# Moving a small weight product, nine small loads, the head masks and the per-batch norms in a two-layer attention and expert kernel

## The chip, the cores and the metric

The kernel runs on one core of one Trainium2 chip. The core has five engines that take their instructions in program order and meet through semaphores: TensorE (PE for matmuls, PEld for its weight loads), VectorE (DVE), ScalarE (ACT), GpSimd (POOL) and SyncE (SP), which only issues DMAs. The metric is the device time in microseconds of one execution; the median of the runs is what counts.

## What is computed

The input x has 8 batches of 512 rows of 128 numbers, all in float32. Two layers follow each other, each of the form x + layernorm(f(layernorm(x))).

```python
def layer1(x):                       # one head of width 128, causal
    q, k, v = rope(x @ wq), rope(x @ wk), x @ wv
    p = softmax(mask(q @ k.T / 128))   # the scale enters once with q and once with k
    return (p @ v) @ wo

def layer2(x):                       # 16 heads of width 4, then 8 experts, 2 chosen per row
    h = rmsnorm(x, g1); c = h @ w_down
    q, k, v = rope(c @ wq), rope(c @ wk), c @ wv
    x = x + softmax(causal(q @ k.T / 2)) @ v @ w_up
    t = rmsnorm(x, g2)
    gate = top2(softmax(t @ router_w))   # two largest, renormalised
    return x + sum(gate[e] * ((silu(t @ w1[e]) * (t @ w3[e])) @ w2[e]) for e in range(8))

x = x + layernorm(layer1(layernorm(x)))
x = x + layernorm(layer2(layernorm(x)))
```

## The kernel before, in words

**Staging.** A batch is 4 tiles of 128 rows. x stays in SBUF (`x_all`), and so do the results of both layers (`h_all`) and all weights. The work has three stages: the "wide" attention of layer 1, batch by batch; the "narrow" attention of layer 2 in units of four heads (class `Unit`, `period`); and the experts. Each stage is begun inside the one before. Most of the order is written out by hand: within `tc.manual_schedule()` each engine's instructions stand in the order in which the Python code emits them, and generators (`prepare`, `fill`, `ffn_front`, `period`) are advanced a step at a time by `step()`. Code outside of such blocks is ordered by a scheduler.

**The start.** SP issues the loads of x (batch 0, then the rope table `ropea`, then batches 1 to 7) and then the expert weights w1s, w3s, w2s (L82 to L111). ACT issues six loads for `wqk`, then `wv` and `wo` (L92 to L100). POOL issues nine small loads, `wdown`, three for `wqkv`, `wup`, `wr`, `g1c`, `g2c`, `ropef` (L391 to L405), and makes the masks: `mask_a` for the wide scores, `mask_q` and `mask_k` for the narrow ones, and `order` for the routing (L409 to L445).

**The norm of x.** `stats_x(b)` (L228) takes the moments of batch b on DVE (`bnst_x`, `mv_x`, `ve_x`), then `root_x` and two small operations for `shift_x` on POOL. `Wide.norm` (L240) has ACT write the four normed tiles `xn`; `Wide.turn` (L253) transposes them on PE and ACT copies `xnT` out of PSUM.

**The projection product.** `fuse_projections` (L208) multiplies wv and wo into `wvo` and takes each row's mean off: a PE transpose, an ACT copy (`wvT`), a PE matmul, three DVE operations. `values` needs `wvo`.

**The wide loop.** `wide_attention` (L994) has 9 rounds (b = 0 to 8) of four phases, with a `yield` after each. In round b, batch b is projected and scored, batch b - 1 gets its probabilities transposed and weighed, and batch b - 2 (only batches 0 to 2) is finished. The methods:

- `project(i)` (L258): PE writes `pq`, DVE multiplies it with the rope table (`two`), POOL adds the halves (`roped`).
- `turn_probs` (L308): PE transposes the probabilities of tiles 0 and 1, then of 2, then of 3 into PSUM (`pT_ps`), and ACT copies each to `pT`.
- `values` (L269): PE writes `pv`, ACT copies `v`. `weigh` (L322): ten PE products `pr`, then on DVE `rinv` and the product into `h_all`.
- `scores(half)` (L282): PE writes two tiles of scores and adds the mask `mask_a`; DVE takes `nmax` and ACT the exponentials `p` of each tile in turn.
- `norm_result` (L343): moments of `h_all` on DVE (`bnst_r`, `ve_r`), then `root_r` on POOL. `add` (L346): four DVE operations that add the normed result to `x_all`. `norm_sum` (L368): moments of the new `x_all` on DVE (`bnst_h`, two `ve`), then four POOL operations for `h_scale`, by which layer 2 norms its input.

The phases of a round were

```
1: norm(b+1), norm_result(b-2), project(b, 0), turn_probs(b-1; 0, 1), project(b, 1)
2: [round 0: fuse_projections], turn_probs(b-1; 2), (3), add(b-2), values(b), norm_sum(b-2)
3: weigh(b-1), stats_x(b+2), turn(b+1), scores(b, first half)
4: scores(b, second half)
```

After each phase the driver (L1052 to L1064) advances other generators: two steps of `prepare` and `fill` in rounds 0 to 2, two steps of `first` in rounds 3 and 4, and from round 5 one step of `first` and of `fronts`; the first narrow scores (`units_begin`) start in phase 3 of round 5.

**The front of layer 2.** `first` is `front_and_rows(0)`. `ffn_front(0)` (L520) norms batch 0 on POOL (`hs`, four operations that need `h_scale`), transposes it on PE (`hT_ps`) with an ACT copy `hT`, projects it on PE (`pqk`, `pvs`) with DVE's product `two` and ACT's copy `vs`, adds the halves on POOL (`rot`), and splits the result there into three bfloat16 parts (`split`, L448: `thirds` and `left`). Six DMAs on SP store the parts to DRAM (`q_dram`, `k_dram`, L569), and `load_rows(0)` (L573) reads them back on SP as `q_rows` and `k_rows`. `Unit.rowwise` (L608) reads these rows for the first narrow scores (`sm`, L617), adds `mask_q` (L600), and DVE takes the maximum (`nm`, L632).

**PSUM.** Three double banks are shared by `pq`, `sc`, `pqk`, `sm` and the like (tag `wide`), and two banks by all transposes, `pv`, `pvs` and `pr` (tag `bank`), in the order of their allocation; one is written again only when its reader is done.

Of the kernel before, what the change touches and what calls it, by code (L numbers as in the profile page):

```python
# [15 lines left out]
P = 128  # L16
# [6 lines left out]
def kernel(  # L23
# [43 lines left out]
    def banks(stack, **bufs):  # L67

        for name, n in bufs.items():
            psum[name] = stack.enter_context(  # L70
                tc.tile_pool(name=f"ps_{name}_{n}", bufs=n, space=bass.MemoryType.PSUM)
            )
# [4 lines left out]
    def bank(name):  # L77
        return psum["bank"].tile([P, 512], F32, tag="bank", name=name)
# [3 lines left out]
    for b in range(B):  # L82
# [4 lines left out]
        if b == 0:  # L87
            ropea = const.tile([P, 2, T], F32, name="ropea")
            nc.sync.dma_start(out=ropea, in_=rope_a)


    wqk = const.tile([P, 2, 2, D], F32, name="wqk")  # L92
    for i, w in enumerate((a_wq, a_wk)):
        nc.scalar.dma_start(out=wqk[:, i, 0, :], in_=w[0])
        nc.scalar.dma_start(out=wqk[:, i, 1, 0 : D // 2], in_=w[0][:, D // 2 : D])
        nc.scalar.dma_start(out=wqk[:, i, 1, D // 2 : D], in_=w[0][:, 0 : D // 2])
    wv = const.tile([P, D], F32, name="wv")
    nc.scalar.dma_start(out=wv, in_=a_wv[0])
    wo = const.tile([P, D], F32, name="wo")
    nc.scalar.dma_start(out=wo, in_=a_wo[0])  # L100

    w1s = const.tile([P, E, F], F32, name="w1s")
    w3s = const.tile([P, E, F], F32, name="w3s")
    w2s = const.tile([P, E, FC, D], F32, name="w2s")
# [103 lines left out]
    def fuse_projections():  # L208
        ps = bank("wvo_ps")
        nc.tensor.transpose(ps[:, :P], wv, ident)  # L210
        wvT = work.tile([P, D], F32, tag="sq", name="wvT", bufs=1)
        nc.scalar.copy(wvT, ps[:, :P])
        ps = bank("wvo_ps2")
        nc.tensor.matmul(ps[:, :P], wvT, wo, start=True, stop=True)
        mean = stat.tile([P, 1], F32, tag="wvo_mean", name="wvo_mean", bufs=1)
        nc.vector.tensor_reduce(mean, ps[:, :P], AX.X, ALU.add)
        nc.vector.tensor_scalar(mean, mean, 1.0 / D, None, ALU.mult)
        nc.vector.tensor_scalar(wvo, ps[:, :P], mean, None, ALU.subtract)
# [9 lines left out]
    def stats_x(b):  # L228
        mv, rstd = ln_stats(x_all, b * NT, "x")
        x_stats[b] = minus_product(mv[:, :, 0], rstd, "shift_x", f"shift_x_{b}"), rstd  # L230
# [151 lines left out]
            h_scale[b] = kept  # L382

    batches = [Wide(b) for b in range(B)]
    with tc.manual_schedule():
        stats_x(0)
        batches[0].norm()
        stats_x(1)


    wdown = const.tile([P, L], F32, name="wdown")  # L391
    nc.gpsimd.dma_start(out=wdown, in_=w_down)
    wqkv = const.tile([L, 3, L], F32, name="wqkv")
    for i, w in enumerate((f_wq, f_wk, f_wv)):
        nc.gpsimd.dma_start(out=wqkv[:, i, :], in_=w)
    wup = const.tile([L, D], F32, name="wup")
    nc.gpsimd.dma_start(out=wup, in_=w_up)
    wr = const.tile([P, E], F32, name="wr")
    nc.gpsimd.dma_start(out=wr, in_=router_w)
    g1c = const.tile([P, 1], F32, name="g1c")  # L400
    nc.gpsimd.dma_start(out=g1c, in_=g1.rearrange("(p o) -> p o", o=1))
    g2c = const.tile([P, 1], F32, name="g2c")
    nc.gpsimd.dma_start(out=g2c, in_=g2.rearrange("(p o) -> p o", o=1))
    ropef = const.tile([P, NT, 2, HD], F32, name="ropef")
    nc.gpsimd.dma_start(out=ropef, in_=rope_f.rearrange("(t p) s d -> p t s d", p=P))  # L405
    ident_bf = const.tile([P, P], BF16, name="ident_bf")
    nc.vector.tensor_copy(ident_bf, ident)

# [9 lines left out]
        channel_multiplier=1,  # L418
    )

    def half_masks(name, sign):


        m = const.tile([P, 2, P], BF16, name=name)
        nc.gpsimd.memset(m, 0.0)
        for i in range(2):
            for h in range(2):
                at = m[i * HR : (i + 1) * HR, h, :]
                nc.gpsimd.affine_select(
                    out=at,  # L430
                    in_=at,
                    compare_op=ALU.is_ge,
                    fill=NEG_BF,
                    base=sign * HR * h,
                    pattern=[[-sign, P]],
                    channel_multiplier=sign,
                )
        return m

    mask_q = half_masks("mask_q", -1)  # L440
    mask_k = half_masks("mask_k", 1)

    order = const.tile([P, E], F32, name="order")
    for e in range(E):
        nc.gpsimd.memset(order[:, e : e + 1], float(E - e))  # L445


    def split(thirds, x, r):  # L448
# [474 lines left out]
    def step(tasks):  # L923
        while tasks:
            try:
                next(tasks[0])
                return True
            except StopIteration:
                tasks.pop(0)
# [64 lines left out]
    def wide_attention():  # L994
        for b in range(B + 1):
            u = batches[b] if b < B else None
            nxt = batches[b + 1] if b + 1 < B else None
            v = batches[b - 1] if b > 0 else None
            w = batches[b - 2] if 0 <= b - 2 < CLOSED else None
            if nxt:  # L1000
                nxt.norm()
            if w:
                w.norm_result()
            if u:
                u.project(0)
            if v:
                v.turn_probs(0, 1)
            if u:
                u.project(1)
            yield  # L1010
            if b == 0:
                fuse_projections()
            if v:
                v.turn_probs(2)
                v.turn_probs(3)
            if w:
                w.add()
            if u:
                u.values()
            if w:  # L1020
                w.norm_sum()
            yield
            if v:
                v.weigh()
            if b + 2 < B:
                stats_x(b + 2)
            if nxt:
                nxt.turn()
            if u:
                u.scores(0)  # L1030
            yield
            if u:
                u.scores(1)
            yield

    def front_and_rows(b):
        yield from ffn_front(b)
        yield
        load_rows(b)
# [4 lines left out]
    units_begin = [period(-2), period(-1)]  # L1044
    begun = period(0)
    with tc.manual_schedule():
        banks(ctx, wide=3)
        with ExitStack() as stage:
            banks(stage, bank=2)
            batches[0].turn()  # L1050
            fronts.append(front_and_rows(1))
            for i, _ in enumerate(wide_attention()):  # L1052
                b = i // 4
                if b < 3:
                    step(setup)
                    step(setup)
                elif b < 5:
                    step(first)
                    step(first)
                else:  # L1060
                    step(first)
                    step(fronts)
                    if b > 5 or i % 4 > 1:
                        step(units_begin)  # L1064
            for _ in range(6):
                step(fronts)
                step(units_begin) or next(begun)
    closes = [batches[b].close() for b in range(CLOSED, B)]
    banks(ctx, bank=1, po=1)
    with tc.manual_schedule():  # L1070
# [84 lines left out]
```

## Time and profile before

| | us |
|---|---|
| median of 4 runs | 798.65 (797.99 to 806.71) |
| the profiled execution | 799.24 |
| its span, first to last instruction | 797.5 |
| granted TensorE clock, mean | 0.988 |
| PE busy in the span | 724.9 (91%) |
| DVE, ACT, POOL busy | 491.1, 326.0, 285.5 |
| first norm of x (ACT `xn`) begins | 8.17 |
| first wide scores (PE `sc`) begin | 21.27 |
| load of the rows of batch 0 issued (SP) | 81.55 |
| first narrow scores (PE `sm`) begin | 91.00 |

A row of the trace in order of time has the start, the busy time, the engine, the line of the code, the operation, out<-in with shape and type, the count, and in brackets the idle time of the engine before it with what ended that. A "q" behind an engine's name means its queue, which issues DMAs. The rows of the windows have, for a stretch of time, the busy time of each engine, the granted clock of TensorE as a fraction of full speed, the mean busy share of the 16 DMA engines and the bytes moved.

### The profile page before, as it was taken

What the parts mean: (1) busy time and instruction counts of PE and PEld (TensorE: products, weight loads), DVE (VectorE), ACT (ScalarE), POOL (GpSimd) and SP (SyncE); (2) the same over time, 40 slices, a digit from 0 to 9 for tenths busy, and PEclk for the clock granted to TensorE, in tenths of its full rate; (3) what the DMA queues carried; (4) which work ended last, traced back from release to release, by engine and by line L of the source; (5) the groups of instructions that cost most, each with busy time, mean ns of one, the idle gap of its engine ahead of it and who ended that gap; (6) DMA issues with size and microseconds to landing.
All of it is one profiled execution on the core that took longest, in us unless ns stands there. A gap on an engine that the chain in (4) does not pass through costs nothing. (4 is left out here: it accounts for less than half of the span.)

```text
span 797.5 us, 15016 instructions
## 1 busy us (share of the span) xinstructions
PE 724.9 (91%) x5886; PEld 431.6 (54%) x5886; DVE 491.1 (62%) x1088; ACT 326.0 (41%) x507; POOL 285.5 (36%) x594
## 2 busy tenths in 40 slices
PE   4989897898988889898899889999999999999994
PEld 1657564444544444444444456665666666666663
DVE  3497667888778776768672246545464545454553
ACT  2554534565656556656567323222222222222220
POOL 7566451455868676757424300101010101010101
PEclk9999999999999999999999899999999999999998
DMA  9121304130403122314000000000000000000000
GB/s 284 34 88 36 85 11 111 37 89 3 110 15 93 31 69 56 100 25 105 20 3 3 0 1 2 14 0 14 1 14 1 14 2 13 1 14 0 14 1 13
DMA packets 29001, 30.36 MB, mean 38 GB/s; under 512 B 6148, under 2 KB 25316, under 8 KB 28932
## 3 DMA queue, kind: packets, MB, share of 16 engines
q0 software_dynamic: 5280, 14.31, 7.0%
q1 hardware_dynamic: 22500, 14.72, 6.5%
q8 instruction: 46, 0.75, 0.4%
q10 hardware_dynamic: 1152, 0.39, 0.2%
q14 instruction: 23, 0.19, 0.1%
HBM read 15.73 MB, written 11.53 MB: 34 GB/s over the span
## 5 line engine op out<-in xcount | busy, mean ns | idle before, releaser
L632 DVE TENSOR_REDUCE nm<-sm 128x2 f32<-128x1024 f32 (+2 forms) x192 | 194.4, 1043 | 35.4 <-PE sm L600 30.5
L696 ACT ACTIVATE pk<-sT 128x1024 f32<-128x1024 f32 x160 | 161.4, 1025 | 79.1 <-PE sT L600 78.6
L874 ACT ACTIVATE sil<-ph 128x512 f32<-128x512 f32 x128 | 76.3, 597 | 251.7 <-PE ph L866 231.3
L875 DVE TENSOR_TENSOR hid<-sil,ph 128x512 f32<-128x512 f32 x128 | 87.4, 687 | 124.0 <-ACT sil L874 124.0
L882 PEld LDWEIGHTS py<-w2s,hid 128*128 128x128 f32 x1024 | 124.2, 192 | 31.9 <-issue 27.4
L866 PE MATMUL ph<-tT_all,w1s 128*128 128x512 f32 x256 | 132.4, 599 | 0.0
L866 PE MATMUL ph<-tT_all,w3s 128*128 128x512 f32 x256 | 131.6, 596 | 0.0
L882 PE MATMUL py<-w2s,hid 128*128 128x128 f32 x1024 | 124.9, 275 | 1.9 <-DVE h_all L891 1.2
L169 POOL TENSOR_TENSOR root_o<-ve_o,half 128x4 f32<-128x4 f32 x8 | 8.2, 1022 | 309.8 <-DVE ve_o L186 309.8
L703 PE MATMUL po<-pk,vpad 128*32 128x512 f32 (+3 forms) x1024 | 97.9, 445 | 0.0
L891 DVE SCALAR_TENSOR_TENSOR h_all<-py,gate_all,h_all 128x128 f32<-128x128 f32 x256 | 72.0, 343 | 30.6 <-PE py L882 30.6
L866 PEld LDWEIGHTS ph<-tT_all,w3s 128*128 128x128 f32 x256 | 49.0, 191 | 62.0 <-issue 62.0
L673 PE MATMUL sT<-q_rows,k_rows 64*128 64x384 bf16 (+3 forms) x512 | 65.0, 299 | 18.7 <-DVE nm L632 13.7
L617 PE MATMUL sm<-k_rows,q_rows 61*128 61x256 bf16 (+3 forms) x512 | 70.9, 303 | 5.5 <-ACT pk L696 3.5
L866 PEld LDWEIGHTS ph<-tT_all,w1s 128*128 128x128 f32 x256 | 44.3, 193 | 31.9 <-issue 21.1
L617 PEld LDWEIGHTS <-q_rows 61*128 61x128 bf16 x512 | 23.6, 94 | 56.1 <-issue 52.0
L600 PE MATMUL sm<-ident_bf,mask_q 64*128 64x64 bf16 (+1 forms) x768 | 49.1, 199 | 0.0
L600 PEld LDWEIGHTS <-mask_q 64*128 64x128 bf16 x768 | 38.8, 96 | 11.7
L600 PE MATMUL sT<-ident_bf,mask_k 64*128 64x128 bf16 (+1 forms) x640 | 43.9, 206 | 0.0
L673 PEld LDWEIGHTS <-k_rows 64*128 64x128 bf16 x512 | 26.2, 93 | 32.3 <-issue 31.7
L451 POOL CAST m<-nm 128x16 bf16<-128x16 f32 x32 | 6.4, 201 | 86.8 <-DVE nm L632 86.7
L600 PEld LDWEIGHTS <-mask_k 64*128 64x128 bf16 x640 | 31.2, 94 | 11.1
(168 smaller groups left out, 844.8 us busy)
## 6 DMA issues: line engine op xcount, KB each, us to landing
q_dram<-thirds POOLq DMA_DIRECT2D x18, 192.0 KB, 3.2
k_dram<-thirds POOLq DMA_DIRECT2D x18, 192.0 KB, 3.7
q_rows<-q_dram POOLq DMA_DIRECT2D x12, 288.0 KB, 5.0
k_rows<-k_dram POOLq DMA_DIRECT2D x12, 288.0 KB, 6.4
q_rows<-m3T SPq DMA_DIRECT2D x192, 2.0 KB
x_all<-in_L_attn_x_dram SPq DMA_DIRECT2D x8, 256.0 KB
out_dram<-y SPq DMA_DIRECT2D x8, 256.0 KB
q_dram<-thirds SPq DMA_DIRECT2D x6, 192.0 KB
```

Source lines behind the costliest of these rows:

```text
L169: nc.gpsimd.tensor_tensor(y, x, half[:, :n], ALU.pow)
L600: nc.tensor.matmul(out[:, :, h * HR : (h + 1) * HR], which[at, h, :], ident_bf[at, at].unsqueeze(1).to_broadcast([HR, out.shape[1], HR]), ...
L617: nc.tensor.matmul(sc[:, i, c * n : (c + 1) * n], self.q[at, 2 * self.g + pair, t * P : n], self.k[at, 2 * self.g + pair, :n], start=(c == 0),
L632: nc.vector.tensor_reduce(self.nm[:, :, pairs[0] : pairs[0] + w, t], sc[:, :, : w * n].rearrange("p i (c n) -> p i c n", n=n), AX.X, ALU.m ...
L673: nc.tensor.matmul(sc[:, i, c : c + n], self.k[at, 2 * self.g + pair, j * P : (j + 1) * P], self.q[at, 2 * self.g + pair, j * P :], start= ...
L696: nc.scalar.activation(p[:, :, :c], sc[:, :, :c], AF.Exp, scale=HD**-0.5)
L703: nc.tensor.matmul(po[h * HP : (h + 1) * HP, j * P :], vpads[self.g][:, j, h, :], self.p[j, h // 2][:, h % 2, :], start=(self.g == 0 and j ...
L866: nc.tensor.matmul(ph[:, i, :], w[:, e, c * P : (c + 1) * P], tT_all[:, b, :], start=True, stop=True,)
L874: nc.scalar.activation(sil, ph[:, 0, :], AF.Silu)
L875: nc.vector.tensor_tensor(hid[:, c, :], sil, ph[:, 1, :], ALU.mult)
L882: nc.tensor.matmul(py[:, t * P : (t + 1) * P], hid[:, c, t * P : (t + 1) * P], w2s[:, e, c, :], start=(c == 0), stop=(c == FC - 1),)
L891: nc.vector.scalar_tensor_tensor(h_all[:, n, :], py[:, t * P : (t + 1) * P], gate_all[:, n, e : e + 1], h_all[:, n, :], ALU.mult, ALU.add,)
```

## The change

- `wv` and `wo` are loaded before `wqk` on ACT's queue.
- The nine small loads are issued by SP, behind x and ahead of the expert weights, and not by POOL.
- `fuse_projections` runs in two parts: its transpose and copy before the first norm, its product and DVE operations after the first `turn`; both stood in phase 2 of round 0.
- `mask_q`, `mask_k` and `order` are made at the end of phase 1 of round 0.
- `norm(b+1)` goes from the head of phase 1 to phase 2, behind the copies of `turn_probs`. `norm_result(b-2)` goes from phase 1 to phase 2, `add(b-2)` from phase 2 to the end of phase 4, behind the scores, and `norm_sum` from phase 2 of the same round to phase 2 of the next.
- `first` starts one phase later (the first phase of round 3 is left out), so that `h_scale` of batch 0 exists; all its steps, `load_rows(0)` too, come one phase later. `units_begin` stays where it was.

From round 7 on the order of every engine's instructions is as before; outside of the wide loop nothing else is changed.

```diff
@@ -88,17 +88,32 @@
             ropea = const.tile([P, 2, T], F32, name="ropea")
             nc.sync.dma_start(out=ropea, in_=rope_a)
 
+    wv = const.tile([P, D], F32, name="wv")
+    nc.scalar.dma_start(out=wv, in_=a_wv[0])
+    wo = const.tile([P, D], F32, name="wo")
+    nc.scalar.dma_start(out=wo, in_=a_wo[0])
 
     wqk = const.tile([P, 2, 2, D], F32, name="wqk")
     for i, w in enumerate((a_wq, a_wk)):
         nc.scalar.dma_start(out=wqk[:, i, 0, :], in_=w[0])
         nc.scalar.dma_start(out=wqk[:, i, 1, 0 : D // 2], in_=w[0][:, D // 2 : D])
         nc.scalar.dma_start(out=wqk[:, i, 1, D // 2 : D], in_=w[0][:, 0 : D // 2])
-    wv = const.tile([P, D], F32, name="wv")
-    nc.scalar.dma_start(out=wv, in_=a_wv[0])
-    wo = const.tile([P, D], F32, name="wo")
-    nc.scalar.dma_start(out=wo, in_=a_wo[0])
-
+
+    wdown = const.tile([P, L], F32, name="wdown")
+    nc.sync.dma_start(out=wdown, in_=w_down)
+    wqkv = const.tile([L, 3, L], F32, name="wqkv")
+    for i, w in enumerate((f_wq, f_wk, f_wv)):
+        nc.sync.dma_start(out=wqkv[:, i, :], in_=w)
+    wup = const.tile([L, D], F32, name="wup")
+    nc.sync.dma_start(out=wup, in_=w_up)
+    wr = const.tile([P, E], F32, name="wr")
+    nc.sync.dma_start(out=wr, in_=router_w)
+    g1c = const.tile([P, 1], F32, name="g1c")
+    nc.sync.dma_start(out=g1c, in_=g1.rearrange("(p o) -> p o", o=1))
+    g2c = const.tile([P, 1], F32, name="g2c")
+    nc.sync.dma_start(out=g2c, in_=g2.rearrange("(p o) -> p o", o=1))
+    ropef = const.tile([P, NT, 2, HD], F32, name="ropef")
+    nc.sync.dma_start(out=ropef, in_=rope_f.rearrange("(t p) s d -> p t s d", p=P))
     w1s = const.tile([P, E, F], F32, name="w1s")
     w3s = const.tile([P, E, F], F32, name="w3s")
     w2s = const.tile([P, E, FC, D], F32, name="w2s")
@@ -210,6 +225,7 @@
         nc.tensor.transpose(ps[:, :P], wv, ident)
         wvT = work.tile([P, D], F32, tag="sq", name="wvT", bufs=1)
         nc.scalar.copy(wvT, ps[:, :P])
+        yield
         ps = bank("wvo_ps2")
         nc.tensor.matmul(ps[:, :P], wvT, wo, start=True, stop=True)
         mean = stat.tile([P, 1], F32, tag="wvo_mean", name="wvo_mean", bufs=1)
@@ -382,27 +398,19 @@
             h_scale[b] = kept
 
     batches = [Wide(b) for b in range(B)]
+    banks(ctx, wide=3)
+    stage = ctx.enter_context(ExitStack())
+    banks(stage, bank=2)
     with tc.manual_schedule():
         stats_x(0)
+        projections = fuse_projections()
+        next(projections)
         batches[0].norm()
         stats_x(1)
-
-
-    wdown = const.tile([P, L], F32, name="wdown")
-    nc.gpsimd.dma_start(out=wdown, in_=w_down)
-    wqkv = const.tile([L, 3, L], F32, name="wqkv")
-    for i, w in enumerate((f_wq, f_wk, f_wv)):
-        nc.gpsimd.dma_start(out=wqkv[:, i, :], in_=w)
-    wup = const.tile([L, D], F32, name="wup")
-    nc.gpsimd.dma_start(out=wup, in_=w_up)
-    wr = const.tile([P, E], F32, name="wr")
-    nc.gpsimd.dma_start(out=wr, in_=router_w)
-    g1c = const.tile([P, 1], F32, name="g1c")
-    nc.gpsimd.dma_start(out=g1c, in_=g1.rearrange("(p o) -> p o", o=1))
-    g2c = const.tile([P, 1], F32, name="g2c")
-    nc.gpsimd.dma_start(out=g2c, in_=g2.rearrange("(p o) -> p o", o=1))
-    ropef = const.tile([P, NT, 2, HD], F32, name="ropef")
-    nc.gpsimd.dma_start(out=ropef, in_=rope_f.rearrange("(t p) s d -> p t s d", p=P))
+        batches[0].turn()
+        next(projections, None)
+
+
     ident_bf = const.tile([P, P], BF16, name="ident_bf")
     nc.vector.tensor_copy(ident_bf, ident)
 
@@ -418,10 +426,9 @@
         channel_multiplier=1,
     )
 
-    def half_masks(name, sign):
-
-
-        m = const.tile([P, 2, P], BF16, name=name)
+    def half_masks(m, sign):
+
+
         nc.gpsimd.memset(m, 0.0)
         for i in range(2):
             for h in range(2):
@@ -435,14 +442,16 @@
                     pattern=[[-sign, P]],
                     channel_multiplier=sign,
                 )
-        return m
-
-    mask_q = half_masks("mask_q", -1)
-    mask_k = half_masks("mask_k", 1)
-
+
+    mask_q = const.tile([P, 2, P], BF16, name="mask_q")
+    mask_k = const.tile([P, 2, P], BF16, name="mask_k")
     order = const.tile([P, E], F32, name="order")
-    for e in range(E):
-        nc.gpsimd.memset(order[:, e : e + 1], float(E - e))
+
+    def late_constants():
+        half_masks(mask_q, -1)
+        half_masks(mask_k, 1)
+        for e in range(E):
+            nc.gpsimd.memset(order[:, e : e + 1], float(E - e))
 
 
     def split(thirds, x, r):
@@ -997,28 +1006,27 @@
             nxt = batches[b + 1] if b + 1 < B else None
             v = batches[b - 1] if b > 0 else None
             w = batches[b - 2] if 0 <= b - 2 < CLOSED else None
-            if nxt:
-                nxt.norm()
-            if w:
-                w.norm_result()
+            summed = batches[b - 3] if 0 <= b - 3 < CLOSED else None
             if u:
                 u.project(0)
             if v:
                 v.turn_probs(0, 1)
             if u:
                 u.project(1)
-            yield
             if b == 0:
-                fuse_projections()
+                late_constants()
+            yield
             if v:
                 v.turn_probs(2)
                 v.turn_probs(3)
             if w:
-                w.add()
+                w.norm_result()
+            if summed:
+                summed.norm_sum()
+            if nxt:
+                nxt.norm()
             if u:
                 u.values()
-            if w:
-                w.norm_sum()
             yield
             if v:
                 v.weigh()
@@ -1031,6 +1039,8 @@
             yield
             if u:
                 u.scores(1)
+            if w:
+                w.add()
             yield
 
     def front_and_rows(b):
@@ -1044,27 +1054,25 @@
     units_begin = [period(-2), period(-1)]
     begun = period(0)
     with tc.manual_schedule():
-        banks(ctx, wide=3)
-        with ExitStack() as stage:
-            banks(stage, bank=2)
-            batches[0].turn()
-            fronts.append(front_and_rows(1))
-            for i, _ in enumerate(wide_attention()):
-                b = i // 4
-                if b < 3:
-                    step(setup)
-                    step(setup)
-                elif b < 5:
+        fronts.append(front_and_rows(1))
+        for i, _ in enumerate(wide_attention()):
+            b = i // 4
+            if b < 3:
+                step(setup)
+                step(setup)
+            elif b < 5:
+                if i % 4 or b > 3:
                     step(first)
                     step(first)
-                else:
-                    step(first)
-                    step(fronts)
-                    if b > 5 or i % 4 > 1:
-                        step(units_begin)
-            for _ in range(6):
+            else:
+                step(first)
                 step(fronts)
-                step(units_begin) or next(begun)
+                if b > 5 or i % 4 > 1:
+                    step(units_begin)
+        for _ in range(6):
+            step(fronts)
+            step(units_begin) or next(begun)
+        stage.close()
     closes = [batches[b].close() for b in range(CLOSED, B)]
     banks(ctx, bank=1, po=1)
     with tc.manual_schedule():
```

More of the change, by code (lines that the diff above doesn't have):

```diff
@@ L1009, in wide_attention @@
                 u.project(1)
+            if b == 0:
+                late_constants()
             yield
-            if b == 0:
-                fuse_projections()
             if v:
```

## The prediction

> **What bounds the kernel now.** I read the page first, then who PE waits for from 0 to 135 us, then the rows of all engines in order of time over that stretch, and last the windows with the granted clock.
>
> ```profile
> PE 724.9 (91%) x5886; PEld 431.6 (54%) x5886; DVE 491.1 (62%) x1088; ACT 326.0 (41%) x507; POOL 285.5 (36%) x594
> ...
> PE   4989897898988889898899889999999999999994
> ...
> PEclk9999999999999999999999899999999999999998
> ```
>
> PE is busy 91% of the span, and near 9 tenths or more everywhere but in the first slices; it issues in program order, so a PE instruction that waits moves all behind it. Only the first 135 us (the wide attention) are reordered by the change; after them the order of every engine is unchanged, so what is won or lost up to about 98 us is carried to the end.
>
> ```profile
> 8.17 1.65 ACT L245 ACTIVATE xn<-x_all,shift_x,root_x 128x128 f32<-128x128 f32 x4 [1.07 <-POOL shift_x L223]
> ...
> 18.69 0.29 DVE L216 TENSOR_REDUCE wvo_mean<-wvo_ps 128x1 f32<-128x128 f32 x1 [1.26 <-PE wvo_ps L214]
> ...
> 21.27 0.64 PE L291 MATMUL sc<-roped,roped 128*128 128x128 f32 x2
> ...
> 55.69 0.66 PE L317 MATMUL pT_ps<-ident,p 128*128 128x128 f32 x4 [1.46 <-ACT pT L320]
> ...
> 58.58 1.65 PE L199 MATMUL hT_ps<-ident,hs 128*128 128x128 f32 x4 [1.34 <-POOL hs L462]
> ...
> 75.23 1.16 POOL L455 TENSOR_TENSOR thirds<-left,thirds 128x512 bf16<-128x512 f32 x1
> ...
> 76.42 0.61 SPq L569 DMA_DIRECT2D k_dram<-thirds  x1
> ...
> 81.55 1.66 SPq L577 DMA_DIRECT2D q_rows<-q_dram  x2
> ...
> 83.33 1.56 SPq L577 DMA_DIRECT2D k_rows<-k_dram  x2
> ...
> 91.00 0.50 PE L617 MATMUL sm<-k_rows,q_rows 61*128 61x512 bf16 x2
> ```
>
> In these rows the first number is the start, the second the busy time, the bracket the idle time before and its releaser. Read: the first norm begins at 8.17, held by POOL; the projection product ends late, so the first scores stand at 21.27; the third probability transpose waits 1.46 for a pT copy, because ACT has the next norm (four xn, 1.65 us) in front of it; the front's transpose hT waits for POOL. The last five rows are a chain that the page does not show: thirds ready at 76.39, six stores, load of q_rows and k_rows from 81.55, first narrow scores (L617) at 91.00 with no wait of note.
>
> ```profile
> 19.00:21.00 2.00, 1.39 (x11) 1.39 (x12) 1.77 (x11) 0.19 (x1) 2.00 (x13) 0.95 1.12 335
> ...
> 21.00:24.00 3.00, 3.00 (x11) 2.04 (x10) 0.36 (x2) 1.44 (x4) 2.11 (x8) 0.50 0.36 101
> ...
> 55.00:60.00 5.00, 2.63 (x16) 1.88 (x17) 4.97 (x17) 2.18 (x5) 4.76 (x7) 1.00 0.24 86
> ...
> 89.00:90.00 1.00, 1.00 (x12) 1.00 (x11) 0.15 (x1) 0.00 (x0) 0.00 (x0) 1.00 0.28 76
> 90.00:91.00 1.00, 1.00 (x9) 0.70 (x8) 1.00 (x4) 0.59 (x1) 0.00 (x0) 1.00 0.09 19
> ```
>
> The columns are busy time of PE, PEld, DVE, ACT and POOL, clock, DMA share and GB/s. DMA of the rows ends in the slice before 91.0: they are there less than 0.8 us before PE wants them. From 55 to 60 DVE is busy 4.97 of 5 us and POOL 4.76: these two, not PE, pace that stretch. From 21 to 24 the clock is 0.50, after a half idle PE.
>
> **The change, part by part** (times worked out for the changed kernel are on the old scale of microseconds; "round b" is pass b of the wide loop).
>
> A. Start. Two POOL DMA issues (0.61, 0.53) leave the gap between root_x and shift_x, one mask select (0.31) enters: root_x ends 6.54, plus 0.31, 0.21, 0.24 and some 0.25 of gaps: 7.55 for the first norm, 0.6 earlier. ACT's table load ends 7.09 and the new wvT copy (0.26) ends before that. The transpose of wv and the product (0.33, 0.49) fit beside the norm and the xnT copy; the three DVE rows of wvo (0.79) run while PE projects. So the row wvo chain (17.14 to 19.56) leaves the path. pq ends 15.55 instead of 16.16, wdT and wg follow as before; xn of batch 1 now stands behind wg on ACT: wg about 17.35, plus 1.65, plus 0.2 for the last transpose: first scores 19.2 instead of 21.27, 2.1 earlier; roped (POOL, about 18.1) is no later. Bounds: -0.6 if a small load holds wg, -2.8 if only roped counts. I take -2.1.
>
> The nine loads on SP: ACT's and SP's issues take 0.33 to 0.51, so nine take 3.0 to 4.6 from 8.81 on, and w1s, w3s, w2s come that much later; their first reader is an expert matmul hundreds of us on: no cost. g1c is the seventh, issued near 11.5; POOL's small loads landed 4.0 to 6.5 after issue, so 15.5 to 18.0, against 16.9 when wg wants it. I take no wait; the late end costs 1.1. The late masks and order (about 3.2 on POOL) go between roped and the wqk4 copies (2.45); root_x of batch 2 then ends near 25.4, its reader xn near 30; the masks' first reader is the row at 91.00. No cost; without that cover up to 3.2.
>
> B. Rounds 1 and 2. With xn behind the pT copies PE's waits for pT (0.78 at 43.27, 1.46 at 55.69, 1.58 at 85.98) go; next late is the exp of p 3 plus one copy (0.47), which leaves 0 to 0.2. In exchange xn and the v copy (1.65 and 0.59) must end before xnT: pv and pr on PE (3.4) hide them, by 0 to 0.3 us. In round 2 add (2.25) and norm_sum (1.6) leave DVE ahead of h_all. pr of round 2 ends 44.45 instead of 47.09; nmax of its first tile 46.5 instead of 49.68; its last nmax 49.7 instead of 52.92. So far -3.2.
>
> C. Round 3, where it turns. add(0) now stands on DVE before the two products, and norm_sum(0) behind them and norm_result(1). One chain from 49.7: add 2.3, two products 2.4, norm_result 1.35, norm_sum 1.4 (57.15), POOL's h_scale 2.45 and four hs 1.9 with gaps (61.65), last hT 0.35: 62.0. In PE's order hT stands between the two halves of the scores, so sc_1 waits behind it; sc_0 is done near 56.7. PE idles some 4.5 us in place of the 1.34 shown. sc_1 still starts at 62.0, not 65.33, but pqk (1.98) and pvs (1.06), which the old order had done by 68, are now behind it.
>
> D. Round 4. sc_1 1.85, two nmax 2.15 (66.0), add(1) 2.3, the front's product 1.22, two_0 1.22: 70.7. add(1) and its product were not in this chain before. Then POOL in order: two roped 2.54, rot 1.3, thirds 0.65, left 1.2, root_r 1.1, h_scale(1) 2.5, second thirds 1.9: 82.0 instead of 76.39, +5.6. h_scale used to run after thirds.
>
> E. The rows. thirds to the load's issue took 5.15 (five stores on SP and their landing), issue to rows 8.65 to 9.45 (the last DMA slice; the sm row itself). So 95.8 to 96.6 against 91.0; middle: +5.2. PE arrives there near 88.8 and finds nothing else to do: a new wait of about 7 us, with sc_1, hT and everything later queued behind the first sm on PE, and DVE and ACT behind them.
>
> F. What comes back. By then DVE and ACT are idle, so the waits before pq at 94.79 and 97.55 (0.53, 0.45) go: -1.0. Nothing further in 98 to 135 has xn in front of a copy.
>
> G. Clock. Half clock from 20.8 to 24.3 costs about 1.7 of PE work; it follows a stretch (17 to 20.5) with PE half busy. That stretch is now fuller: 0 or -1.7, I take -0.9. The new waits (4.5 and 7) are emptier than that stretch: each 0 to +1.7. I take +1.1 for sc_1 in round 3 and +1.2 behind the first sm, where part falls in other waits. Sum +1.4; ends -1.7 and +3.4.
>
> [...] No row here has a 7 us gap with PE work right behind it.
>
> Sum: +5.2 -1.0 +1.4 = +5.6. Span 797.5 becomes 803.1; the profiled execution's 799.24 (1.74 outside the span) 804.8. It stood 0.6 above the median 798.65 of the four, so the median forecast is 804.3.
>
> **Rivals.** 1, other side: the rows are in time. It decides at thirds ready by about 74.5 (88.8 less 14.2), 7.5 sooner than I work out; that needs hs early enough not to hold PE in round 3. For it: every earlier step gains, and hs waited little before (1.34). Against: DVE's 4.97 of 5 in that very stretch. PE then comes to sm at 88.8 instead of 91.0: -2.2, 796.4; with the early cold stretch gone too, 794.7.
> 2, the clock becomes the bound: both waits cost 1.7 and the cold stretch at 21 stays: +3.4 in place of +1.4, 806.3; more if a second cold window follows. For it: 0.50 after a half idle PE; against: 55 to 60 had PE 2.63 busy of 5 and kept 1.00.
> 3, the small loads do not do what they are for: behind 2.6 MB of x_all and ropea on SP, g1c lands at 18.0 or later and holds wg, xn and the first scores; thirds and the rows move with it: +1.1, 805.4. For it: SP's issues of w1s were held up to 2.5 us; against: the data in front is through by about 11.5 at 320 GB/s.
>
> **How the numbers follow.** Forecast 0.55 (from 800.5 to 807 by its own bounds: thirds 79.5 to 83.5 and the clock), rival 1 0.22, rival 2 0.13, rival 3 0.10. Range: 795 holds most of rival 1, 808.5 the forecast with the start at -0.6 and both cold stretches whole (804.3 + 1.5 + 2.0, rounded up). About 1% is what a measurement can tell from no change: below 790.7 needs rival 1 and more, 0.02; above 806.6 lies a sixth of the forecast (0.09), most of rival 2 (0.09) and a third of rival 3 (0.03): 0.21; the rest, 0.77, is within 1%.
>
> **What would show it.** A: first scores near 19.2, wg not held by a DMA. B: no PE wait on pT copies. C: PE waiting some 4 us on POOL hs before hT, near 57 to 62. D: second thirds ending near 82. E: the first sm waiting about 7 us on the rows' DMA, starting near 96. G: 0.50 behind both waits. Wrong if sm starts before 91, if hT waits less than 2 us, or if PE's idle time up to 100 us shrinks.

## The result and the profile after

| | before | after |
|---|---|---|
| median of all runs, us | 800.81 (68 runs, 796.05 to 806.71) | 804.42 (44 runs, 802.27 to 809.60) |
| the profiled execution, us | 799.24 | 808.14 |
| its span, us, and granted clock | 797.5, 0.988 | 806.4, 0.974 |

The ratio of after to before is 1.0039, with a 95% interval of 1.0027 to 1.0052: 3.1 us more (the two medians differ by 3.6), within the 1% that was called no change. The profiled execution of after stands 3.7 us above its median; a part of its length, told below, is the clock's and not the change's.

The page of after, its busy line of the engines, PE's slices and the clock's:

```profile
PE 732.7 (91%) x5886; PEld 434.7 (54%) x5886; DVE 488.2 (61%) x1088; ACT 325.7 (40%) x507; POOL 280.1 (35%) x585
...
PE   5989598888989888989889889999999999999994
...
PEclk9999799999999999999999899999999999999998
```

One slice is 20 us. The fifth slice of PE (80 to 100) has fallen from 9 to 5, and the clock there to 7: the largest loss is in one place. PE's waits up to 135 us, the whole list but for six of 0.5 us and less and two at the start (columns: sum, times, longest); then, from the same list of before, its waits for pT copies:

```profile
PE sm L626 <- issue: 8.3, 1, 8.3
...
PE hT_ps L214 <- POOL hs L471: 2.1, 1, 2.1
PE pT_ps L333 <- ACT pT L336: 1.4, 1, 1.4
PE sm L626 <- DMA k_rows<-k_dram: 1.2, 1, 1.2
```
```profile
PE pT_ps L317 <- ACT pT L320: 5.2, 4, 1.6
```

Of these four waits one is left (at 131 us). The 9.5 us at the first narrow scores (8.3 and 1.2) were not there at all. The rows of after that answer to those shown of before, in order of time, and last the first projection of round 6 in before:

```profile
7.39 1.65 ACT L261 ACTIVATE xn<-x_all,shift_x,root_x 128x128 f32<-128x128 f32 x4
...
18.53 0.39 PE L307 MATMUL sc<-roped,roped 128*128 128x128 f32 x2
...
47.58 1.13 DVE L366 SCALAR_TENSOR_TENSOR x_all<-h_all,root_r,x_all 128x128 f32<-128x128 f32 x4
...
56.88 1.77 PE L214 MATMUL hT_ps<-ident,hs 128*128 128x128 f32 x4 [2.09 <-POOL hs L471]
58.45 1.49 PE L307 MATMUL sc<-roped,roped 128*128 128x384 f32 x2
...
73.70 1.64 POOL L393 TENSOR_TENSOR h_scale<-ve,half 128x8 f32<-128x8 f32 x1
...
76.76 1.16 POOL L464 TENSOR_TENSOR thirds<-left,thirds 128x512 bf16<-128x512 f32 x1
...
84.39 1.67 SPq L586 DMA_DIRECT2D q_rows<-q_dram  x2
86.17 1.56 SPq L586 DMA_DIRECT2D k_rows<-k_dram  x2
...
92.69 0.58 PE L626 MATMUL sm<-k_rows,q_rows 61*128 61x512 bf16 x1 [8.26 <-issue]
94.51 0.58 PE L626 MATMUL sm<-k_rows,q_rows 61*128 61x512 bf16 x1 [1.24 <-DMA k_rows<-k_dram]
...
95.13 1.65 PE L307 MATMUL sc<-roped,roped 128*128 128x384 f32 x2
...
99.37 1.98 PE L278 MATMUL pq<-xnT,wqk 128*128 128x512 f32 x4
```
```profile
94.79 1.98 PE L262 MATMUL pq<-xnT,wqk 128*128 128x512 f32 x4 [0.53 <-DVE nm L632]
```

Read it as a race. The first scores start at 18.53 in place of 21.27 and PE, done with the first scores of round 5, stands at the first sm at 84.44 in place of 91.00: it is 6.6 us ahead. But thirds end at 77.92 and not at 76.39, the load is issued at 84.39 and not at 81.55, and the second half of the rows is there at 94.5. PE's lead is waited away, and the projections of round 6 start at 99.37, where before had them at 94.79: 4.6 us late, 4.0 by 117 us.

How the clock goes through that wait, microsecond by microsecond (columns: busy time of PE, PEld, DVE, ACT, POOL, then the granted clock, DMA share, GB/s):

```profile
84.00:85.00 1.00, 0.44 (x3) 0.10 (x1) 1.00 (x9) 0.24 (x1) 1.00 (x1) 1.00 0.03 9
...
87.00:88.00 1.00, 0.00 (x0) 0.00 (x0) 0.00 (x0) 0.01 (x1) 0.92 (x2) 1.00 0.74 153
88.00:89.00 1.00, 0.00 (x0) 0.00 (x0) 0.00 (x0) 0.00 (x0) 0.91 (x3) 0.52 0.81 204
...
97.00:98.00 1.00, 1.00 (x2) 0.27 (x2) 0.00 (x0) 0.00 (x0) 0.00 (x0) 0.50 0.00 0
98.00:99.00 1.00, 1.00 (x8) 0.44 (x7) 0.35 (x1) 0.00 (x0) 0.00 (x0) 0.86 0.00 0
```

PE goes idle at 84.44; the clock halves at 88.04, 3.6 us later (0.52 in that slice is 0.04 us at full and 0.96 at half), and is whole again at 98.28 (0.86: 0.28 at half), 3.8 us after PE went to work without a break at 94.51.

### The profile page after: what moved, and what is told of

Read it like the earlier page. It is cut to its first block, busy times and chain, and to the rows that moved or that the text cites. A ratio compares the mean times of both kernels' runs of the same rounds, so it can differ in the third digit from the quotient of the medians.

```text
span 806.4 us, 15016 instructions
## 1 busy us (share of the span) xinstructions
PE 732.7 (91%) x5886; PEld 434.7 (54%) x5886; DVE 488.2 (61%) x1088; ACT 325.7 (40%) x507; POOL 280.1 (35%) x585
## 5 line engine op out<-in xcount | busy, mean ns | idle before, releaser
L705 ACT ACTIVATE pk<-sT 128x1024 f32<-128x1024 f32 x160 | 161.2, 1025 | 81.9 <-PE sT L609 81.5
L609 PE MATMUL sm<-ident_bf,mask_q 64*128 64x64 bf16 (+1 forms) x768 | 49.7, 201 | 0.0
```

What stands on the lines that cost most here:

```text
L609: nc.tensor.matmul(out[:, :, h * HR : (h + 1) * HR], which[at, h, :], ident_bf[at, at].unsqueeze(1).to_broadcast([HR, out.shape[1], HR]), ...
L705: nc.scalar.activation(p[:, :, :c], sc[:, :, :c], AF.Exp, scale=HD**-0.5)
```

## The experiments

All ratios are to the kernel before on the same chip, with 95% intervals. Every kernel runs the whole computation; e7 and e11 add products whose results are written over.

| | what it is | median us | ratio |
|---|---|---|---|
| e2 | start alone | 799.14 | 0.9966 (0.9935 to 0.9996) |
| e3 | wide norms and later `first` alone | 806.95 | 1.0073 (1.0049 to 1.0097) |
| e4 | later `first` alone | 807.05 | 1.0073 (1.0044 to 1.0102) |
| e1 | after, narrow scores two phases later | 796.59 | 0.9943 (0.9920 to 0.9965) |
| e10 | before, narrow scores two phases later | 797.49 | 0.9970 (0.9944 to 0.9996) |
| e12 | e2 and e10 together | 796.75 | 0.9948 (0.9919 to 0.9976) |
| e5 | start and norm of x alone | 799.24 | 0.9983 (0.9959 to 1.0006) |
| e6 | after, norm_sum a phase earlier | 804.79 | 1.0066 (1.0038 to 1.0095) |
| e8 | e5, hT a phase later | 798.50 | 0.9986 (0.9960 to 1.0011) |
| e9 | e8 and e1 together | 794.66 | 0.9934 (0.9908 to 0.9960) |
| e7 | after, products in the wait | 803.98 | 1.0026 (0.9993 to 1.0058) |
| e11 | after, more products in the wait | 804.17 | 1.0043 (1.0014 to 1.0072) |

The theory: the rows that come later cost the time, since PE can do nothing else at the first sm. The rivals: the start or the loads on SP cost it; DVE and POOL bound it whatever PE waits for; the clock does.

**Taking the change apart: e2, e3, e4.** e2 has the new start with the old loop; e3 the new loop with the old start; e4 is before with one line changed:

```diff
-                    step(first)
-                    step(first)
+                    if i % 4 or b > 3:
+                        step(first)
+                        step(first)
```

> The kernel before with the start of the changed one alone (wvo product in two parts, small loads on SP, late masks); the per-batch norms and first as before. Theory: the first scores start near 18.5 and the half-clock stretch at 21 to 24 is gone; that is carried to the rows, which come as much earlier, so the first sm waits less than 1 us: 2 to 3 us under the kernel before, ratio 0.9965 to 0.9975. Rival (the loads on SP or the late masks on POOL cost something later): not under the kernel before, ratio 1.000 or more.

> The kernel before with the moves of the wide norms and the later start of first alone; start as before. Theory: everything as in the changed kernel but for the start's gain, so 2 to 3.5 us over the changed kernel: first sm near 96 to 98 behind a wait of 8 to 10 us, ratio to the kernel before 1.006 to 1.009. Rival (the start is what costs): ratio 1.000 to 1.003.

> The kernel before with first begun one phase later and nothing else. Theory: hs, hT, pqk and thirds come a phase later in program order, thirds end some 3 us later (79 to 80), the rows with them; they came less than 1 us before PE wanted them, so PE idles 2.5 to 3.5 us at the first sm (near 94): ratio 1.003 to 1.005. Rival (the chain to thirds is paced by DVE and POOL and not by where the steps stand): thirds less than 1 us later, no wait, ratio 0.999 to 1.001.

The window from 21 to 24 of e2 (columns as above) and its first sm:

```profile
21.00:24.00 3.00, 2.53 (x15) 1.54 (x14) 2.09 (x5) 1.38 (x6) 2.78 (x21) 1.00 1.10 343
```
```profile
88.54 0.39 PE L626 MATMUL sm<-k_rows,q_rows 61*128 61x512 bf16 x2
```

The first sm starts 2.5 us sooner, without a wait. The half-clock stretch (0.50 in before) is gone as well, but that is not shown to be the start's doing: of the kernels with the old start, e10 has it (0.56) and e3 and e4 do not. The same window of e3:

```profile
21.00:24.00 3.00, 3.00 (x18) 1.99 (x17) 1.31 (x7) 1.66 (x5) 2.42 (x10) 1.00 0.56 157
```

The start gains 0.34%, as expected. The new loop costs 0.73%, also as expected, and the product 0.9966 x 1.0073 = 1.0039 is the ratio of the whole change: the two parts add up, each known to 0.3%. But e4, which moves `first` by a phase and nothing else, costs 0.73% too, where 0.3 to 0.5% was expected. Its second thirds on POOL, then its first sm on PE:

```profile
82.69 1.16 POOL L455 TENSOR_TENSOR thirds<-left,thirds 128x512 bf16<-128x512 f32 x1
```
```profile
97.06 0.58 PE L617 MATMUL sm<-k_rows,q_rows 61*128 61x512 bf16 x1 [4.33 <-issue]
98.57 0.58 PE L617 MATMUL sm<-k_rows,q_rows 61*128 61x512 bf16 x1 [0.93 <-DMA k_rows<-k_dram]
```

Thirds end at 83.85, 7.5 us late and not 3; PE waits 5.3 us, and comes late as well, with a colder clock behind its wait for hs (2.2 us): 0.91 and 0.92 in the windows from 60 to 80, and the second scores of round 3 (128x512) took 1.83 for 1.08. So one line alone costs as much as the whole new loop, within these 0.3%, and the moves of the wide norms bring nothing net in e3.

**Covering the wait: e1, e10, e12.** The edit to after (the same two conditions in e10 to before, in e12 to e2):

```diff
-                if b > 5 or i % 4 > 1:
+                if b > 5:
+                    step(units_begin)
+                if i in (24, 25):
                     step(units_begin)
```

> The changed kernel, but the first narrow scores come two phases later in program order (behind the projections of round 6), and the step count is caught up in those two phases. Theory (the late rows cost the time): PE has about 7 us of other work (second scores, hT, two pq, pT) while the rows land near 92.7 to 94.5, so the 9.5 us of idling at the first sm shrink to 1 to 3 us, and the matmuls behind it are no longer at half clock; 1 to 2 us are given back because two steps of narrow scores stand close together. Time 797 to 800, 4 to 7 us under the changed kernel. Rival (the rows are not what costs, DVE and POOL are the bound there): the idle time only moves, time 803 to 806.

> The kernel before with only the first narrow scores two phases later. Theory (e1 gained because it covered the wait for the rows): the kernel before waits nothing there, so nothing is won, ratio 0.998 to 1.002. Rival (the later place gains by itself, by two steps of narrow scores in one phase): ratio 0.996 or less, and then only part of e1's gain is the rows'.

> e2 and e10 together: the new start and the first narrow scores two phases later, the wide norms and first at their old places. It tells what the moves of the wide norms are worth once the wait for the rows is covered. Theory (start and later narrow scores add up, 0.9966 and 0.9970, and the moves of the norms bring nothing): ratio to the kernel before 0.992 to 0.9955, level with e1 and e9. Rival (the norms' gain of 5 us by round 3 reaches the end in e1): not under 0.9965.

PE's waits in e1 at the first sm:

```profile
PE sm L626 <- issue: 1.1, 1, 1.1
PE sm L626 <- DMA k_rows<-k_dram: 1.1, 1, 1.1
```

They shrink from 9.5 to 2.1 us, the clock stays at 1.00 from 65 to 110, and the ratio falls from 1.0039 to 0.9943: the rows were what cost. That is 7.7 us (0.96% of 800.8), a little over the 4 to 7 expected, but not all of it is the wait's: the same edit in e10, where nothing waited, is worth 0.30% or 2.4 us. That lies between the theory's nothing and the rival's 0.4%, and its interval (0.3 to 4.5 us) reaches both. About 5 us are then left for the wait and its clock, uncertain by some 2. In e10 PE's two waits before pq, 0.53 and 0.45 us on DVE and ACT, are gone, which is the part of it that the trace shows. e12, without any move of the wide norms, came in as its theory had it and is level with e1: what these moves gain up to round 3 shows at the end of no kernel here, as far as 0.3% can tell.

**Why the norms' gain does not arrive: e5, e6, e8, e9.** e5 is after with norm_result, add, norm_sum and `first` put back, so that only the start and the place of `norm(b+1)` differ from before. e6 is after with

```diff
-            if summed:
-                summed.norm_sum()
...
             if w:
                 w.add()
+                w.norm_sum()
```

and `first` as in before. e8 is e5 with one step of `first` left out in phase 2 of round 3 and made up for in round 4; e9 adds the edit of e1.

> The changed kernel with norm_result, add and norm_sum and the start of first back at the places that they have in the kernel before; the new start and the norm of x behind the pT copies stay. Theory (only the later rows cost, everything else gains): the waits of PE for pT copies in rounds 1 to 5 go (6 us in five waits in the kernel with the new start alone), of which 1 to 3 us reach the first sm; the rows come as early as with the start alone, the first sm waits less than 1.5 us: ratio to the kernel before 0.991 to 0.995. Rival (DVE paces these rounds, the pT waits were cover for something else): as the start alone, ratio 0.996 to 0.998.

> The changed kernel, but norm_sum stands right behind add at the end of phase 4, not in phase 2 of the next round, and first starts in phase 1 of round 3 as in the kernel before. Theory: h_scale of batch 0 is then made on POOL before the roped of round 3, hs does not wait for it, thirds end near 73 and not 77.9, the rows land near 88 to 90, and PE waits less than 3 us at the first sm in place of 9.5: ratio to the kernel before 0.989 to 0.994. Rival (h_scale in front of roped on POOL delays the scores of round 3, and norm_sum in front of the products delays DVE): a wait of 1.5 us or more for roped in each of rounds 3 to 5, ratio 0.996 or more.

> The kernel of e5 (new start, norm of x behind the pT copies, all else at its old place), with hT and pqk of batch 0 one phase later, behind the transposes and first scores of round 3, and the step count caught up in round 4. Theory: in e5 the waits for pT copies only moved into one wait of 2.7 us at hT, which with four slow transposes left PE nearly idle for 4.3 us and made pr take 4.5 in place of 2.4 at half clock; with pr, xnT and sc in front of it, hT waits less than 1.5 us, the clock stays at 1.00 from 55 to 60, and the time is 2 to 4 us under e5: ratio to the kernel before 0.992 to 0.996. Rival (POOL's chain to the rows paces it and only the place of the wait changes): the first sm waits 3 us or more on the rows instead, ratio 0.997 to 1.000.

> e8 and e1 together: hT one phase later and the first narrow scores two phases later. Theory: no wait for the rows over 1 us and none at hT over 1.5 us, no slice under 0.9 of the clock before 100 us: ratio to the kernel before 0.986 to 0.992, under both kernels. Rival (DVE and POOL are the bound by then): as e1, 0.993 to 0.996.

All four fell short of their theories (e9 came out in its rival's range), and by the same mechanism. In e5 the waits for pT copies are gone up to 100 us, and PE is at hT (it stands behind pv there) at 52.48; e6 the same, only longer. The rows of e5, then its clock, then PE's rows of e6 and one of POOL:

```profile
55.20 1.79 PE L214 MATMUL hT_ps<-ident,hs 128*128 128x128 f32 x4 [2.72 <-POOL hs L471]
56.79 4.48 PE L343 MATMUL pr<-v,pT 128*128 128x128 f32 x20
```
```profile
56.00:57.00 1.00, 1.00 (x4) 0.67 (x4) 0.67 (x8) 0.00 (x0) 0.76 (x3) 0.50 0.00 1
```
```profile
56.11 1.76 PE L214 MATMUL hT_ps<-ident,hs 128*128 128x128 f32 x4 [4.19 <-POOL hs L471]
57.66 4.31 PE L343 MATMUL pr<-v,pT 128*128 128x128 f32 x20
...
79.31 0.80 PE L307 MATMUL sc<-roped,roped 128*128 128x128 f32 x2 [3.19 <-POOL roped L282]
```
```profile
71.23 1.67 POOL L393 TENSOR_TENSOR h_scale<-ve,half 128x8 f32<-128x8 f32 x1 [5.44 <-DVE ve L391]
```

PE arrives early and waits for POOL's hs; four transposes, each behind its own hs tile, make the stretch 4.3 us long (52.48 to 56.79), the clock halves at about 55.2, 2.7 us into it (0.58 in the slice from 55 to 56, then 0.50 until 62), and pr takes 4.48 where before took 2.40. What the pT waits gave is paid back with interest: the next scores start at 61.91, in e2 at 60.29. In e6 a second wait follows: h_scale of batch 1 now stands on POOL in front of rot, thirds, left and roped, and itself waits 5.44 us for DVE's norm_sum; PE waits 3.19 us for roped, and the clock is 0.50 again from 80 to 85. The rival of e6 had named this wait, for each of rounds 3 to 5; it came in round 4 alone. So e6 lost 0.66% where a gain of 0.6% and more was expected.

e8 takes the wait at hT away, and it comes back one instruction later, at pqk. On ACT the hT copy stands behind the exponentials, these behind DVE's nmax, and DVE had add (until 55.44), norm_sum, h_all and the moments of x in front of that, until 58.87. ACT's rows of e8, then PE's:

```profile
59.24 0.37 ACT L315 ACTIVATE p<-sc,nmax 128x128 f32<-128x128 f32 x1 [3.33 <-DVE nmax L313]
...
60.65 0.57 ACT L538 COPY hT<-hT_ps 128x512 f32<-128x512 f32 x1
```
```profile
61.28 2.76 PE L543 MATMUL pqk<-hT,wqk 128*128 128x512 f32 x4 [2.60 <-ACT hT L538]
```

The clock has 0.74 from 60 to 65 and the time is e5's. The rival was right in its main point (only the place of the wait changes), though it had named the wrong place. e9, with both edits, has the lowest median here, 0.66% under before and so under both kernels, but its interval holds e1's and e12's ratios.

**The clock's share: e7 and e11.** Products of 128x512 in float32 into the PSUM tile of the first sm, in front of it (six in e7, eight in e11 and one between its halves):

```diff
+            if self.n == 0 and (t, pairs) == (NT - 1, (0,)):
+                for _ in range(8):
+                    nc.tensor.matmul(
+                        sc[:, 0, :], ident, x_all[:, 0:NT, :], start=True, stop=True
+                    )
...
```

> The changed kernel with six products of 128x512 float32 more (identity by x_all, written over by what follows) in front of the first sm, where PE only waits for the rows. It measures the clock's share. Theory (the idling costs about 1.7 us beyond itself): the clock stays above 0.9 from 90 to 100 in place of 0.50 and 0.67, the sc behind the first sm take 0.91 and 1.08 and not 1.65 and 1.88, and the start of the pq of round 6 moves from 99.4 to about 97.7; time 1 to 2 us under the changed kernel, near 802.5 to 803.5. Rival (the slow matmuls have another cause): the same durations and a start of pq at 99.2 or later.

> As e7, but with eight products in front of the first sm and one between its two halves, so that no gap of over 1.2 us is left in the stretch (e7 left gaps of 2.44 and 1.06 us and its clock fell to 0.50 all the same). Theory (near-idle stretches of 3.5 us and more cost the clock): 0.9 or more from 90 to 100, sc behind the first sm in 0.91 and 1.08, pq of round 6 at 97.5 to 98.5; time 1.5 to 2 us under the changed kernel, near 802 to 803. Rival (something other than the idling takes the clock): sc in 1.65 and 1.88 again.

e7 told nothing: its products ended at 91.18, gaps of 2.44 and 1.06 us were left around half a microsecond of work, and the clock was 0.50 from 95 to 100 again. e11 closed the gaps:

```profile
92.78 0.39 PE L635 MATMUL sm<-k_rows,q_rows 61*128 61x512 bf16 x1
...
93.16 0.91 PE L307 MATMUL sc<-roped,roped 128*128 128x384 f32 x2
93.97 1.08 PE L307 MATMUL sc<-roped,roped 128*128 128x512 f32 x2
...
95.86 1.98 PE L278 MATMUL pq<-xnT,wqk 128*128 128x512 f32 x4
```
```profile
95.00:100.00 5.00, 5.00 (x25) 2.30 (x25) 3.51 (x4) 2.31 (x6) 0.47 (x1) 1.00 0.00 0
```

From the second half of the first sm to pq are 3.08 us, where after has 4.86 (94.51 to 99.37): the half clock behind this wait costs 1.8 us. Idling is its cause: e11 differs from after in the added products alone, and has 1.00 from 90 to 100 where after has 0.50 (90 to 95) and 0.67 (95 to 100). The 3.5 us and more of its theory lie under the stretches measured in after (PE idle for 3.6 us until the clock fell) and e5 (4.3 us); they are no border, since one of 2.8 us lost the clock in e10 (last section). (The rest of e11's lead of 3.5 us at pq is not the clock: its rows were there by 92.78, in after at 94.51.) The whole time of e11 does not show it: 1.0043 is level with after's 1.0039, though the expected 1.002 lies within the interval. In the profiled execution e11 keeps this lead at the first transposed maximum (122.2 to 125.7). Later it has a stretch that no other kernel here shows, 335 to 340, with the clock at 0.70, and lacks one that after has, 235 to 245 (0.82 and 0.50). Whether the added products have to do with these is open.

## Why the prediction came out, step by step

The mechanism and the place were right: after the change a wait of the first sm on the rows takes the place of all that is won before it. Of the steps several were mis-sized, in both directions.

That the median of 804.42 meets the 804.3 so closely is luck. The forecast was +5.6 us on a median of four runs, 798.65; the median of all runs of before is 800.81, 2.2 higher, and the change is +3.6. In the forecast's own terms the sum comes to +4.3: the rows +3.5 and not +5.2, the two waits before pq -1.0 as expected, the clock behind sm +1.8. The trace has 4.6 at pq and 4.0 at 117 us. The clock's other two terms (-0.9 and +1.1) lie ahead of the first sm, where PE now waits, and reach the end only through the time of the rows.

None of the three signs of being wrong came: sm starts at 92.69 and not before 91, PE's idle time up to 100 us grew from 19.6 to 21.4, and hT waits 2.09, just over the limit of 2.

- **A, right, a little small.** First scores at 18.53 (19.2 expected); the first norm at 7.39 (7.55). wg waited for PE and for no load. SP's nine issues took 0.43 to 0.98 each (8.67 to 14.24, 5.6 us; 3.0 to 4.6 expected), which nothing waited for. e2 gives the start's worth, 0.34% or 2.7 us.
- **B, right, too small.** The first nmax of round 2 starts at 44.41 and not at 46.5 (49.68 before): 5.3 us gained in place of 3.2. Of the 5.3, the start alone brings 2.4 (e2 has this nmax at 47.25), near the 2.1 expected. The other 2.8 come with the moves of the norms, which were sized at 1.1.
- **C and D, wrong in size.** The four add took 1.13 and not 2.3: POOL was idle then (46.3 to 49.9), while in e5, beside roped and hs on POOL, the same four take 2.28. So the chain began at 47.6 and not at 49.7, h_scale was done at 56.27, hT waited 2.09 and not 4.5, and the second thirds ended at 77.92: +1.5 instead of +5.6. The order of the chain was right: h_scale of batch 1 does stand in front of the second thirds, and takes 2.4 us there.
- **E, right in kind, with two errors that partly cancel.** thirds ended 4.1 sooner than expected, but thirds to issue took 6.47, not 5.15, and issue to the last rows 10.1, not 8.65 to 9.45: rows at 94.5 instead of 96.2. And PE, gaining in B and C, came at 84.4 and not at 88.8. So the wait is 9.5 and not 7, and the second half of sm is 3.5 late rather than 5.2.
- **F, right:** the waits of 0.53 and 0.45 before pq are gone.
- **G, right in sign, one of three in size.** Behind hT the sc of round 3 took 1.49 and 1.53 for 0.86 and 1.08 (clock 0.66 from 58 to 62): 1.1 us, as expected. Behind sm 1.8 (e11) and not 1.2: that is just over the 1.7 which G allowed each wait at most. The stretch at 21 to 24 was taken at -0.9, as it is fuller now. It is gone in after, but e3 and e4 lack it with the old start, and e2, 2.0 ahead at the first scores and 2.4 at the nmax of round 2, gains at most 0.4 by it.
- **Rival 1** (rows in time) needed thirds by 74.5 with PE at 88.8; they came at 77.92 with PE at 84.4. **Rival 2** was half right: both waits cost clock (1.1 and 1.8), the stretch at 21 did not stay. **Rival 3** did not occur.

"Carried to the end" holds up to the clock's chance: after is 4.0 late at 117 us and 8.7 at the first expert matmul in its profiled execution (455.1 against 446.4), with dips of the clock at 132 to 136 (0.57), 240 to 260 (0.87) and 405 to 410 (0.66) that before did not have; e3 and e7 lack the first of them too (1.00 from 130 to 140). The medians differ by 3.6.

One thing stays open: why thirds to load took 1.3 us longer than before. (Load to rows, 0.6 longer, lies within the scatter of the other runs: 9.2 in e1, 10.2 in e6.) The waits of SP show the stores landing later (3.0 us instead of 1.6 behind the last issue). e1, e3, e7 and e11, with the same order, have it too (6.1 to 6.5 from thirds to issue), the other kernels do not (5.1 to 5.2). In the last microsecond before the load the mean share of the 16 DMA engines is 0.05 to 0.06 in after (83.5 to 84.5), about one engine at work, and in before 1.00 until just before the load (81.0 to 81.5): a part of one store comes late. Why it does was not tried.

## What to carry to other kernels

Before moving an early stage forward, find the first instruction whose input comes by a chain of its own (here POOL, DRAM and back), and compare the two arrivals: a gain on one side that makes the other a phase later is lost whole, and one line (e4, 0.73%) can cost more than the other moves win (e2, 0.34%). If the consumer's place is free, move it behind the arrival (e1, e12: 0.5% under before) rather than hasten the producer. An early arrival on PE is not free either: the waits that it made here cost 1.1 us (after, at hT) to 2.1 us (e5, at hT, on pr alone) of clock behind them.

## What the runs showed of the hardware

- **The clock fell behind nearly idle stretches too, not only behind empty ones, and the runs show no sharp border.** 2.8 us with four transposes, from pv to pr, kept 1.00 in before (the first row) and lost it in e10 (the other two; 0.59 from 61 to 62, 0.50 from 62 to 63), whose order is the same up to there. Behind empty stretches it fell 2.7 us after PE went idle in e5 and 3.6 in after. At the start, behind a half-busy stretch from 17 to 20 (PE 1.35 of 3 us), before had 0.50 from 21 to 24; e4, behind an emptier one from 18 to 21 (1.13 of 3), kept 1.00.

```profile
60.07 2.40 PE L327 MATMUL pr<-v,pT 128*128 128x128 f32 x20
```
```profile
59.49 1.65 PE L199 MATMUL hT_ps<-ident,hs 128*128 128x128 f32 x4 [1.33 <-POOL hs L462]
60.97 4.03 PE L327 MATMUL pr<-v,pT 128*128 128x128 f32 x20
```

- **The scatter of before goes with the clock.** The lower a run's mean clock, the longer it takes, with a little overlap: 796 us at 0.992, 798 to 799 at 0.988, 801 to 803 at 0.984, 804 to 806 at 0.980. e9, which has 0.72 from 60 to 65 in its profile, runs within 792.8 to 796.2. That stretches like those above make the scatter was not tested.
- **DVE's four add of 128x128 took 1.13 us with POOL idle and 2.28 with POOL at work** (after at 47.58, shown above, and e5), the same instructions. Between them lies 1.63, in after at 77.22, where POOL's last thirds overlap only their first 0.7 us.

```profile
53.00 2.28 DVE L366 SCALAR_TENSOR_TENSOR x_all<-h_all,root_r,x_all 128x128 f32<-128x128 f32 x4
```

  The prediction's 2.3 for add is the time beside a busy POOL (2.25 in before at 44.01, with roped on POOL until 45.58), taken for a place where POOL had nothing to do. Why the four take longer beside POOL's work, no run shows.
